# An attention and expert layer on one core: the order of work in the front

## The chip, the cores and the metric

The kernel runs on one core of a Trainium2 chip. The metric is the device time of one execution in microseconds. The core has TensorE (PE in the profile; its weight loads are listed apart as PEld), VectorE (DVE), ScalarE (ACT), GpSimd (POOL) and SyncE (SP), which only issues transfers here. Each engine works through its own list of instructions in order and waits where data of another engine is missing. Transfers are issued from the queues of SP, ACT and POOL.

## What is computed

```python
xn = layernorm(x)                                   # x: 8 sequences x 1024 tokens x 256
# causal linear attention, 16 heads of 16
q = elu(xn @ Wq.T) + 1 ; k = elu(xn @ Wk.T) + 1 ; v = xn @ Wv.T
out = einsum(q, cumsum(k v)) / clip(einsum(q, cumsum(k)), 1e-6)
attn = out @ Wo.T
# 8 experts, the best 2 of each token
logits = xn @ Wr + br
weights, experts = top_k(logits, 2) ; weights = softmax(weights)
ffn = sum over the two of weight * (silu(xn @ W1[e]) * (xn @ W3[e])) @ W2[e]
result = x + attn + ffn
```

All is in float32. The experts run on gathered rows alone: a tile is 128 rows of one expert.

## The kernel before

**Blocks and tiles.** The 8192 tokens are 16 blocks of 512 (four chunks of 128). Attention goes block by block. The experts go tile by tile: the first 4 blocks (FB) make a first list of 25 full tiles (N1), so that expert work can start before all tokens are routed; the other tiles come from a second list.

**The front** is everything up to the first expert tile. It is written in one `manual_schedule` section (L1084 to L1169), in which VectorE, ScalarE, TensorE and GpSimd keep the order in which the program names their instructions. The work comes from generators: each `next(...)` issues the instructions up to the next `yield`. After the section the framework's planner chooses the order; `in_order` pins single instructions to the program's order.

**What the front does.** WARMING (L104) matmuls without use run first on TensorE (L1087). `first_moments(t)` (L284) makes the statistics of block t on VectorE (bn_stats L290, bn_aggr L292, variance plus epsilon L296), raises them to the power -0.5 on GpSimd (L297) and makes the negative mean times that (the column "less", L299). `normalise(t)` (L333) applies it, chunks 0 and 2 on VectorE and 1 and 3 on ScalarE, all four of block 3 on VectorE, all of later blocks on ScalarE. `turn(t)` (L349) transposes the block on TensorE (L358) and copies it out on ScalarE (L363). `logits(t)` (L372) multiplies by the router's weights. The logits of four blocks are copied, turned (L1113 to L1119) and added up in `add_logits` (lg_all, L389).

`route(0, FB)` (L412) finds the two best experts of each token on VectorE, counts on TensorE how many rows of an expert stand before each token (`cnt_ps`, L465), and from that gives every row its place in the lists (`slot`, L486). Then come the softmax weights (L490 to L494), which go into the table `tab`; the table is written to DRAM by a transfer on SP (L1192).

`first_batch()` (L634) turns places into lists. For each of 32 columns (16 chunks, first and second expert) a 128 x 128 mask is made that has a one, or the token's number, where a row's place is. The masks of the first experts are made on VectorE in groups of four (`at_places`, L593), those of the second on ScalarE (two passes each, L672 and L676) for columns 0 to 7 and on GpSimd (L652) for 8 to 15. TensorE sums them (`sum_ps`, L706); ScalarE copies the sums (`sums4`, L713), a small matmul folds them (L715), and `tokens` (L616) makes the row numbers on VectorE. GpSimd then gathers rows and table entries of each tile (`ffn_load`, L1214).

**Block 0's attention** is partly in the front: `project_q`, `project_k`, `project_v` (L816 to L857), with `elu1` (two ScalarE passes for the exponential, one VectorE combine), and `mask_q` (L827), which masks q for pairs of heads on ScalarE. Their results stand in four PSUM buffers of the pool `ps_mm`.

**Queues.** SP takes, in program order: blocks 0 to 3, the small weights, blocks 4 and 5, w2, copies of the turned blocks, acc copies of x, the table, then tile 0's weights (`ffn_weights`, L1283, two transfers of 512 KB), more acc copies, tile 1's weights, the blocks 6 and 7, wo, the blocks 8 and 9, then tile 2's weights and so on. The weights have five buffers, so the second half of tile 2's waits until tile 0's first half was used. From tile 1 on, SP reads the expert's number from `te_late`, a copy that GpSimd makes behind tile 0's gather. Blocks 6 to 15 are normalised later, two at a time (`moments(t, 2)`, L302): VectorE reads both blocks, and block t's `normalise` needs the result.

**After the front**, a loop over tiles j (L1389) does one `ffn_step` and some attention steps. `ffn_turn(j)` turns a tile's gathered and normalised rows on TensorE, `ffn_hidden` makes the gate and up products (`gu_ps`, L1307) and their combination hT, `ffn_out` multiplies by w2 (`y_ps`, L1326).

Of the kernel before, what the change touches and what calls it, by code (L numbers as in the profile page):

```python
# [46 lines left out]
F32 = mybir.dt.float32  # L47
# [7 lines left out]
P = 128  # L55
# [9 lines left out]
def tile_attention_moe(  # L65
# [38 lines left out]
    WARMING = 14  # L104
# [155 lines left out]
    nc.gpsimd.memset(va, 0.0)  # L260
# [3 lines left out]
    nc.gpsimd.memset(own_of, 0.0)  # L264
# [3 lines left out]
    nc.gpsimd.tensor_scalar(upto_neg, before, -1.0, None, ALU.add)  # L268
    base_row = iota("base_row", E, ROWS, 0, 0)

    for o in range(KC):
        nc.gpsimd.tensor_copy(own_of[:, o, o * HALF : (o + 1) * HALF], own)
# [11 lines left out]
    def first_moments(t):  # L284
# [3 lines left out]
        for c in range(NCH + 1):  # L288
            if c < NCH:
                nc.vector.bn_stats(st[:, c, :], xbs[t][:, c, :])  # L290
            if c > 0:
                nc.vector.bn_aggr(mv[:, c - 1, :], st[:, c - 1, :])  # L292
            if t == FB and c == 1:
                yield
# [111 lines left out]
    nc.gpsimd.memset(new, 1.0)  # L406
    nc.gpsimd.memset(new[:, :, 0:1], 0.0)
# [4 lines left out]
    def route(a, b):  # L412
# [40 lines left out]

        reset = new[:, :, 0:n]
# [18 lines left out]
        )  # L473
        yield
# [14 lines left out]
        den2 = work("den2", n)  # L489
        nc.vector.tensor_scalar(den2, diff, 1.0, None, ALU.add)  # L490
        wt = tab[:, tiles, 0]
        nc.vector.reciprocal(wt, den2)
        second = slice(NT + a * NCH, NT + b * NCH)
        nc.vector.tensor_tensor(tab[:, second, 0], diff, wt, ALU.mult)  # L494
        if a > 0:
            nc.vector.tensor_copy(tab[:, second, 1:3], tab[:, tiles, 1:3])
        yield
# [136 lines left out]
    def first_batch():  # L634
# [7 lines left out]
        late = FT - 2 * PART  # L642
# [3 lines left out]
        less_place = f_one.tile([P, late], F32, name="less_place")  # L646
        nc.scalar.mul(less_place, place[:, 1, 0:late], -1.0)
        place_f = f_one.tile([P, 2 * PART], F32, name="place_f")
        nc.gpsimd.tensor_copy(place_f, place[:, 1, late:FT])
        late_at = [masked.tile([P, PART, P], F32, tag="s_sb", name="late_at") for _ in range(2)]  # L650
        for i in range(2 * PART):
            nc.gpsimd.tensor_scalar(  # L652
                late_at[i // PART][:, i % PART, :], cols, place_f[:, i : i + 1],
                number1[:, FT + late + i : FT + late + i + 1], ALU.is_equal, ALU.mult,
            )
        upto = add_up(sizes(False), "upto1")
# [13 lines left out]
        mid_at = [masked.tile([P, PART, P], F32, tag="s_sb", name="mid_at") for _ in range(2)]  # L670
        for i in range(late):
            nc.scalar.activation(  # L672
                mid_at[i // PART][:, i % PART, :], cols, AF.Square,
                bias=less_place[:, i : i + 1],
            )
            nc.scalar.activation(  # L676
                mid_at[i // PART][:, i % PART, :], mid_at[i // PART][:, i % PART, :], AF.Relu,
                bias=number1[:, FT + i : FT + i + 1], scale=from_last[:, i : i + 1],
            )

# [9 lines left out]
        yield  # L690
        sum_ps = ps_y.tile([P, P], F32, tag="y", name="sum_ps")
        groups = [(late_at, 2), (None, 0), (mid_at, 0), (mid_at, 1), (None, 1), (late_at, 3)]
        groups += [(None, 2), (None, 3)]
        for n, (made, g) in enumerate(groups):
            if made is None:
# [4 lines left out]
            else:  # L700
                at = made[g % 2]
            if n == 1:
                yield
            for i in range(PART):
                c = N1 * ((0 if made is None else FT) + g * PART + i)
# [78 lines left out]
    def elu1(dst, z):  # L784

        neg = two.tile([P, TB], F32, tag="neg", name="neg")
# [40 lines left out]
    def mask_q(t, o):  # L827
        qT, qm = blocks[t][0:2]
        for a in range(2):
            nc.scalar.mul(qm[:, o, a, :], qT[:, o, :], par[:, a : a + 1])  # L830

    def project_kv(t, c, a):
        z = ps_mm.tile([P, 2, H], F32, tag="mm", name="zkv"[:2] + "kv"[a])
# [8 lines left out]
    def project_k(t, c):  # L842
# [3 lines left out]
            kn[:, c : c + 2, :].rearrange("p c h -> p (c h)"), z.rearrange("p c h -> p (c h)")  # L846
# [237 lines left out]
    with tc.manual_schedule(engines={EN.DVE, EN.Activation, EN.PE, EN.Pool}):  # L1084
# [9 lines left out]
        next(parts[0])  # L1094
        for t in range(FB):
            next(parts[t + 1])
            next(parts[t])
            normalise(t)
            if t == 2:
                nc.scalar.copy(lgT4[:, 0, :], lg_ps.pop(0))  # L1100
            turn(t)
# [6 lines left out]
            else:  # L1108
                lg_ps[t - 1] = logits(t - 1)
        next(parts[FB])  # L1110
        lg4 = ps_t.tile([P, FB * P], F32, tag="t", name="lg4")
        for t in range(1, FB - 1):
            nc.vector.tensor_copy(lgT4[:, t, :], lg_ps.pop(t))  # L1113
        for t in range(FB - 1):
            nc.tensor.transpose(lg4[:, bass.ts(t, P)], lgT4[:, t, :], ident)
        next(constants)
        next(parts[FB])
        nc.scalar.copy(lgT4[:, FB - 1, :], logits(FB - 1))
        nc.tensor.transpose(lg4[:, bass.ts(FB - 1, P)], lgT4[:, FB - 1, :], ident)  # L1119
# [5 lines left out]
        turn(FB)  # L1125
        routing = route(0, FB)
# [3 lines left out]
        next(qs[0])  # L1130
        next(routing)
        listing = first_batch()
        next(listing)
        next(listing)
        lg_t = logits(FB)
        ks = [project_k(0, c) for c in range(0, NCH, 2)]
        for k in ks:
            next(k)
        lgT = f_two.tile([P, P], F32, tag="lgT", name="lgT")
        nc.scalar.copy(lgT, lg_t)  # L1140
# [3 lines left out]
        next(routing)  # L1144
        next(vs[0])
        mask_q(0, 0)
# [348 lines left out]
```

## Time and profile before

| | us |
|---|---|
| median of 3 runs | 1266.21 (1262.2 to 1268.4) |
| the profiled execution, its own time | 1262.54 |
| its span, first to last instruction | 1260.7 |
| block 0 normalised, start | 9.71 |
| logits of four blocks added (lg_all), start | 21.91 |
| sums of the first list copied, start | 41.53 |
| tile 0's rows gathered, issue | 44.33 |
| first expert matmul (gu_ps L1307), start | 49.99 |
| block 6's rows read by VectorE, start | 54.81 |
| TensorE busy, 0 to 50 / 50 to 140 | 36.22 / 85.90 |
| TensorE busy, 500 to 1100 | 600.00 |

The profile is one execution. Times of instructions count from the start of the span. A group's line gives the line in the code, the engine, what is written and what is read, how often, the busy time and the idle time ahead of it with the instruction that ended it. The chain of waits is followed back from the last instruction, so it names at each moment the work for which the end was waiting. In a table of stages, each row gives a stretch of time, its length, the busy time of PE, PEld, DVE, ACT and POOL in it, the clock that TensorE was granted (1.00 is full), the DMA engines' share, and GB/s. A busy PE is not a PE at full clock.

### The profile page before, as it was taken

The numbers are of one execution on the slowest core, as the hardware profiler recorded it, in microseconds if no ns is written. First come the engines' busy times: TensorE is split into PE (matmuls) and PEld (weight loads), VectorE is DVE, ScalarE is ACT, GpSimd is POOL, SyncE is SP. The second block draws the span as 40 slices with busy tenths as digits, with TensorE's granted clock in tenths as the row PEclk, the third lists the DMA queues.
The fourth block names the chain that finished last, engine by engine and source line by source line (L and its number), as shares of the span: only waits on it lengthen the run. The fifth ranks groups of instructions, "written<-read, shape, count | busy, mean of one in ns | idle before, by whom it ended". The sixth has DMA issues, their size and how long they took to land.

```text
span 1260.7 us, 29753 instructions
## 1 busy us (share of the span) xinstructions
PE 1217.8 (97%) x11460; PEld 1058.2 (84%) x11460; DVE 674.5 (54%) x1541; ACT 560.9 (44%) x1068; POOL 522.2 (41%) x460
## 2 busy tenths in 40 slices
PE   7799999999999999999999999999999999999994
PEld 5578887787898989988888989989888889899884
DVE  7677589864354554545453545545453545445451
ACT  5666475461534526262624426262626344252620
POOL 4734233233334544443535444444443444443422
PEclk9899999999999999999999999999999999999998
DMA  9798565557788796979799797879896877969782
GB/s 334 278 288 255 174 192 118 181 157 224 212 191 196 173 235 155 228 176 219 161 196 207 164 224 155 219 180 207 184 215 161 197 193 168 218 157 231 166 177 35
DMA packets 203934, 245.84 MB, mean 195 GB/s; under 512 B 72946, under 2 KB 127858, under 8 KB 203506
## 3 DMA queue, kind: packets, MB, share of 16 engines
q1 hardware_dynamic: 161010, 191.79, 52.5%
q0 software_dynamic: 38032, 43.22, 24.2%
q10 hardware_dynamic: 4752, 8.91, 2.1%
q8 instruction: 94, 1.54, 0.5%
q14 instruction: 46, 0.38, 0.1%
HBM read 187.91 MB, written 44.29 MB: 184 GB/s over the span
## 4 chain that ended last, share of the span: by engine, by line
PE 87%; DVE 5%; ACT 3%; DMA 3%; issue 1%; POOL 0%; SPq 0%; POOLq 0%; DVEq 0%; ACTq 0%
PE gu_ps L1307 37%; PE y_ps L1326 17%; PE s_ps L937 5%; PE o_ps L974 5%; PE a_ps L1016 5%; PE zq L820 4%; PE zkv L836 4%; PE zkk L836 4%; PE o_ps L956 2%; DMA xb<-in_x_dram 1%; PE tp L358 1%; DMA out_dram<-y,dst_i 1%; PE tp L883 1%; PE lg_ps L378 1%; DMA out_dram<-at 1%
## 5 line engine op out<-in xcount | busy, mean ns | idle before, releaser
L1307 PE MATMUL gu_ps<-xgT,w 128*128 128x128 f32 x4224 | 509.3, 277 | 0.5 <-ACT xgT L1270 0.5
L1307 PEld LDWEIGHTS gu_ps<-xgT,w 128*128 128x128 f32 x4224 | 489.1, 192 | 20.0 <-issue 14.4
L1337 POOL DMA_INDIRECT out_dram<-y,dst_i x107 | 175.2, 1638 | 328.3 <-DVE s_sb L944 103.3
L1326 PE MATMUL y_ps<-w_sb,hT 128*128 x1056 | 251.0, 380 | 1.8 <-DVE hT L1318 1.6
L1217 POOL DMA_INDIRECT xg<-in_x_dram,src_i x132 | 129.1, 978 | 240.1 <-DVE half L1240 109.9
L1326 PEld LDWEIGHTS y_ps<-w_sb,hT 128*128 128x128 f32 x1056 | 190.4, 191 | 23.6 <-DVE hT L1318 2.0
L944 DVE TENSOR_TENSOR s_sb<-s_ps,causal 128x512 f32<-128x512 f32 x256 | 159.8, 682 | 81.5 <-PE s_ps L937 75.2
L1315 ACT ACTIVATE hT<-gu_ps 128x512 f32<-128x512 f32 x132 | 78.8, 597 | 277.1 <-PE gu_ps L1307 207.5
L1222 POOL DMA_INDIRECT entry<-tab_d,of_i x107 | 106.4, 995 | 42.3 <-issue 31.4
L1318 DVE TENSOR_TENSOR hT<-gu_ps,hT 128x512 f32<-128x512 f32 x132 | 90.3, 684 | 61.9 <-PE gu_ps L1307 33.0
L1240 DVE COPY half<-xg 128x512 uint16<-128x512 uint16 x105 | 47.5, 453 | 134.9 <-ACT xg L1230 134.9
L1333 DVE TENSOR_SCALAR y<-y_ps,entry 128x256 f32<-128x256 f32 x132 | 63.6, 482 | 99.8 <-PE y_ps L1326 99.5
L1021 ACT COPY at<-a_ps 128x256 f32<-128x256 f32 x64 | 23.8, 372 | 172.1 <-PE a_ps L1016 123.7
L937 PE MATMUL s_ps<-qm,kT 32*128 32x256 f32 x1024 | 85.4, 404 | 0.5 <-DVE hT L1318 0.4
L1258 ACT COPY xgT<-halfT 128x512 uint16<-128x512 uint16 x105 | 79.7, 759 | 6.5 <-DMA halfT<-half 6.5
L1230 ACT ACTIVATE xg<-xg,entry 128x256 f32<-128x256 f32 x132 | 78.6, 596 | 4.1 <-DMA entry<-tab_d,num_i 3.4
L1016 PE MATMUL a_ps<-wo_sb,oT 128*128 128x256 f32 x256 | 68.2, 387 | 3.0 <-DVE oT L991 2.7
L974 PE MATMUL o_ps<-s_sb,va 128*32 128x128 f32 x2048 | 69.9, 276 | 0.0
L974 PEld LDWEIGHTS o_ps<-s_sb,va 128*32 128x32 f32 x2048 | 52.3, 109 | 17.9 <-issue 15.3
L937 PEld LDWEIGHTS s_ps<-qm,kT 32*128 32x128 f32 x1024 | 50.6, 184 | 18.6 <-issue 9.3
L1337 POOL DMA_INDIRECT acc_d<-y,src_i x25 | 40.9, 1637 | 53.0 <-DVE y L1333 15.1
L836 PE MATMUL zkv<-wkv_sb,xnT 128*128 128x256 f32 x256 | 59.6, 386 | 0.0
(228 smaller groups left out, 1353.9 us busy)
## 6 DMA issues: line engine op xcount, KB each, us to landing
w<-in_w_dram SPq DMA_DIRECT2D x264, 512.0 KB
rden<-over SPq DMA_DIRECT2D x128, 64.0 KB
xnT<-xnT_d SPq DMA_DIRECT2D x15, 512.0 KB
out_dram<-at POOLq DMA_DIRECT2D x13, 512.0 KB
out_dram<-in_x_dram SPq DMA_DIRECT2D x12, 512.0 KB
xnT_d<-xnT ACTq DMA_DIRECT2D x11, 512.0 KB
xb<-in_x_dram SPq DMA_DIRECT2D x9, 512.0 KB
w_sb<-in_w_dram SPq DMA_DIRECT2D x4, 1024.0 KB
```

The lines of the kernel that those rows point to most:

```text
L836: nc.tensor.matmul(z[:, i, :], lhsT=xnTs[t][:, k, bass.ts(c + i, P)], rhs=wkv_sb[:, k, a, :], start=(k == 0), stop=(k == KC - 1),)
L937: nc.tensor.matmul(s_ps[r][:, hh].rearrange("p a l -> p (a l)"), lhsT=kT[rows, hh, span], rhs=qm[rows, hh, :, span], start=True, stop=True,)
L944: last_masked[0] = nc.vector.tensor_tensor(sm, s_ps[r].rearrange("p k a l -> p (k a) l"), causal_b, ALU.mult)
L974: nc.tensor.matmul(o_ps[32 * r : 32 * r + 32, hh, :], lhsT=va[:, c, 4 * hh + r, a, :], rhs=s_sb[r][:, 2 * hh + a, :], start=(first and a = ...
L1016: nc.tensor.matmul(a_ps, lhsT=oT[:, hh, :], rhs=wo_sb[:, hh, :], start=(hh == 0), stop=(hh == 1),)
L1217: rows = nc.gpsimd.indirect_dma_start(out=xg[j], out_offset=None, in_=x_rows[:, :], in_offset=bass.IndirectOffsetOnAxis(ap=src_i[:, i : i ...
L1222: nc.gpsimd.indirect_dma_start(out=entry[j], out_offset=None, in_=table[:, :], in_offset=bass.IndirectOffsetOnAxis(ap=num_i[:, i : i + 1], ...
L1258: nc.scalar.copy(xgT[j].bitcast(U16).rearrange("p k (l b) -> p b k l", b=2), halves.pop(j).rearrange("p (b k) l -> p b k l", b=2),)
L1307: done = nc.tensor.matmul(ps[:, i, :], lhsT=w13[:, k, bass.ts(i, P)], rhs=xgT[j][:, k, :], start=(k == 0), stop=(k == KC - 1),)
L1318: nc.vector.tensor_tensor(hT, gu[1], hT, ALU.mult)
L1326: done = nc.tensor.matmul(y_ps, lhsT=hT[:, i, :], rhs=w2_sb[:, bass.ds(e * (IC * H) + i * H, H)], start=(i == 0), stop=(i == IC - 1),)
L1337: nc.gpsimd.indirect_dma_start(out=rows[:, :], out_offset=bass.IndirectOffsetOnAxis(ap=dst_i[:, i : i + 1], axis=0), in_=ys.pop(j), in_off ...
```

## The change

Nothing that is computed changes. It moves instructions of the front, and changes where some are made:

- WARMING is 18 instead of 14. Eight memsets, copies and conversions that GpSimd made early (va, own_of, upto_neg, new) go into `later_constants()`, called behind the last power.
- `first_moments` now pauses at chunk 2 of every block. Block 0's power is asked for at once and block 0 is normalised ahead of block 1's statistics; later blocks are normalised between the two parts of the next block's statistics. The copies of logits 1 and 2 stand in other places, and logits 3 come ahead of the turning of logits 2.
- The softmax weights are made while the counts run.
- Of the second experts' masks, GpSimd makes columns 8 to 14 and VectorE column 15.
- The exponentials of k follow ScalarE's masks, ahead of the sums; their scratch is the tile of kT. The sums are summed and copied in one piece, ahead of value copies, lgT's copy and the silu table load. q's combines follow the row numbers on VectorE. `mask_q` of block 0 follows the turning of tile 0.
- Four matmuls without use follow block 4's turn; 14 narrow ones (128 columns) replace the 3 wide ones (512) before the first tile.
- On SP, only block 6 is loaded behind tile 1's weights; blocks 7, 8 and 9 follow the weights of tiles 2, 3 and 4, and wo follows block 7.
- The transposes of tile 1's rows are pinned in order.

```diff
-    WARMING = 14
+    BY_ACT = 8
+    BY_POOL = 15
+    WARMING = 18
...
-            if t == FB and c == 1:
+            if c == NCH - 2:
                 yield
...
-    nc.gpsimd.memset(new, 1.0)
-    nc.gpsimd.memset(new[:, :, 0:1], 0.0)
+    def later_constants():
+        nc.gpsimd.memset(new, 1.0)
+        nc.gpsimd.memset(new[:, :, 0:1], 0.0)
+        nc.gpsimd.tensor_scalar(upto_neg, before, -1.0, None, ALU.add)
+        nc.gpsimd.memset(own_of, 0.0)
+        for o in range(KC):
+            nc.gpsimd.tensor_copy(own_of[:, o, o * HALF : (o + 1) * HALF], own)
+        nc.gpsimd.memset(va, 0.0)
...
+        if a == 0:
+            weights_of()
         yield
...
+        for i in range(BY_ACT, BY_POOL):
+            at_one(nc.gpsimd, made[i // PART][:, i % PART, :], FT + i, place_p[:, i : i + 1])
...
-        groups = [(late_at, 2), (None, 0), (mid_at, 0), (mid_at, 1), (None, 1), (late_at, 3)]
-        groups += [(None, 2), (None, 3)]
+        groups = [(1, 2), (1, 0), (0, 0), (0, 1), (1, 1), (0, 2), (0, 3), (1, 3)]
...
-        z = ps_mm.tile([P, 2, H], F32, tag="mm", name="zkv"[:2] + "kv"[a])
+        if t == 0 and a == 1:
+            z = ps_t.tile([P, 2, H], F32, tag="t", name="zv")
+        else:
+            z = ps_mm.tile([P, 2, H], F32, tag="mm", name="zkv"[:2] + "kv"[a])
...
         next(parts[0])
+        next(parts[0])
         for t in range(FB):
-            next(parts[t + 1])
+            if t > 0:
+                next(parts[t + 1])
             next(parts[t])
             normalise(t)
+            if t == 0:
+                next(parts[t + 1])
             if t == 2:
                 nc.scalar.copy(lgT4[:, 0, :], lg_ps.pop(0))
+            elif t == FB - 1:
+                nc.vector.tensor_copy(lgT4[:, 1, :], lg_ps.pop(1))
+            next(parts[t + 1])
             turn(t)
...
+        later_constants()
+        nc.vector.tensor_copy(lgT4[:, 2, :], lg_ps.pop(2))
+        next(constants)
         next(parts[FB])
         lg4 = ps_t.tile([P, FB * P], F32, tag="t", name="lg4")
-        for t in range(1, FB - 1):
-            nc.vector.tensor_copy(lgT4[:, t, :], lg_ps.pop(t))
-        for t in range(FB - 1):
+        for t in range(2):
             nc.tensor.transpose(lg4[:, bass.ts(t, P)], lgT4[:, t, :], ident)
...
+        def keep_busy(n, *cols_of):
+            for _ in range(n):
+                idle_ps = ps_mm.tile([P, TB], F32, tag="mm", name="idle_ps")
+                nc.tensor.matmul(idle_ps[:, 0:P], lhsT=ident, rhs=causal, start=True, stop=True)
+
+        keep_busy(4)
         routing = route(0, FB)
         next(routing)
         next(qs[1])
         next(routing)
-        next(qs[0])
         next(routing)
         listing = first_batch()
+        ks = [project_k(0, c) for c in range(0, NCH, 2)]
         next(listing)
         next(listing)
+        next(ks[0])
+        next(ks[1])
         lg_t = logits(FB)
-        ks = [project_k(0, c) for c in range(0, NCH, 2)]
-        for k in ks:
-            next(k)
-        lgT = f_two.tile([P, P], F32, tag="lgT", name="lgT")
-        nc.scalar.copy(lgT, lg_t)
         vs = [project_v(0, c) for c in range(0, NCH, 2)]
         next(vs[0])
         next(listing)
-        next(routing)
+        next(listing)
+        for q in qs:
+            next(q)
+        next(constants)
+        next(vs[1])
+        lgT = f_two.tile([P, P], F32, tag="lgT", name="lgT")
+        nc.scalar.copy(lgT, lg_t)
+        nc.scalar.activation(warm, ones[:, 0:1], AF.Silu)
+        for k in ks:
+            next(k)
         next(vs[0])
-        mask_q(0, 0)
-        next(listing)
-        next(qs[1])
-        next(constants)
-        next(listing)
-        nc.scalar.activation(warm, ones[:, 0:1], AF.Silu)
-        mask_q(0, 1)
         next(vs[1])
...
         attend_upto(3, False)
-
-        for _ in range(3):
-            idle_ps = ps_mm.tile([P, TB], F32, tag="mm", name="idle_ps")
-            nc.tensor.matmul(
-                idle_ps, lhsT=ident, rhs=blocks[0][0][:, 0, :], start=True, stop=True
-            )
+        keep_busy(14)
         next(routing)
...
+        if j < 3:
+            load_x(FB + 3 + j, nc.sync)
+        if j == 0:
+            in_order(nc.sync.dma_start(out=wo_sb, in_=woT.rearrange("(k p) o -> p k o", p=P)))
...
     ffn_turn(0)
+    for o in range(KC):
+        mask_q(0, o)
     ffn_weights(1)
-    for t in range(FB + 2, FB + 6):
-        load_x(t, nc.sync)
-        if t == FB + 3:
-            in_order(
-                nc.sync.dma_start(out=wo_sb, in_=woT.rearrange("(k p) o -> p k o", p=P))
-            )
+    load_x(FB + 2, nc.sync)
```

## The prediction

> **What bounds the kernel now.** I read the page's totals first, then the chain that ended last in its first 60 us, the engines' timelines of that stretch, and the table of stages for clock and busy time.
>
> ```profile
> span 1260.7 us, 29753 instructions
> PE 1217.8 (97%) x11460; PEld 1058.2 (84%) x11460; DVE 674.5 (54%) x1541; ACT 560.9 (44%) x1068; POOL 522.2 (41%) x460
> ```
>
> TensorE (PE) is busy 97% of the span. Between 60 and 1226 us it hardly waits, so what the front saves reaches the end one for one, and nothing else in this change can. The chain through the front (start, length, what):
>
> ```profile
> 1.83 5.79 DMA xb<-in_x_dram
> ...
> 9.71 0.42 DVE xb L338
> ...
> 10.17 0.65 PE tp L358 x3
> ...
> 21.91 0.30 DVE lg_all L389
> ...
> 39.08 0.63 ACT neg L788
> ...
> 40.41 1.23 ACT qm L830 x2
> 41.64 0.17 ACT sums L713
> ...
> 47.01 7.77 DMA xb<-in_x_dram
> 54.81 0.43 DVE st L312
> ```
>
> Three places matter. Block 0 is normalised at 9.71, after block 1's statistics (7.64 to 9.60), though its own variance was done at 5.69. The sums of the first list are complete at 39.32 and copied only at 41.53, because ScalarE first does a second exponential pair, a value copy and a masking of q. And VectorE stands from 51.3 to 54.81 for block 6's rows, with block 5's last step queued behind. What that does to PE (stage: length, busy time by engine, granted clock, DMA share, GB/s):
>
> ```profile
> 39.32:41.85 2.53, 0.00 (x1) 0.00 (x0) 0.00 (x0) 2.51 (x8) 0.00 (x0) 1.00 0.45 159
> 42.10:45.55 3.45, 3.45 (x11) 2.66 (x11) 1.84 (x6) 2.43 (x4) 2.42 (x3) 0.55 1.04 398
> 54.45:55.99 1.54, 0.00 (x2) 0.00 (x1) 1.18 (x3) 0.65 (x2) 1.24 (x2) 1.00 1.08 391
> 55.99:59.11 3.12, 2.54 (x8) 1.58 (x9) 3.12 (x11) 3.12 (x7) 2.81 (x2) 0.51 1.08 379
> 59.11:65.43 6.32, 6.32 (x50) 5.10 (x50) 5.88 (x29) 1.46 (x4) 2.60 (x3) 0.70 1.06 402
> ```
>
> PE idles, and right after each idle stretch the granted clock falls to about half.
>
> **Part 1, statistics and constants.** Block 0's power now follows its variance: ready at 5.69, POOL is free because the 3.1 us of constants (va 1.79, upto_neg 0.55, and smaller ones) go behind the powers. Power 1.01 to 1.05, less 0.16: normalising starts at about 7.1 instead of 9.71. The warm-up grows by 4 matmuls of two passes; warm passes take 0.11, cold ones 0.23, so it ends at 7.5 to 8.0 and no longer leaves the 3.5 us gap, after which the clock was 0.50 (12 to 14 us). But VectorE sets the pace afterwards: it starts on block 1 at 7.8, each block costs 2.7 (statistics and variance 1.94, less and normalising 0.76) as before, and three rather than two chunks of block 4 now come ahead of block 3's normalising. That starts at 16.4 to 17.0, against 16.68: nothing won by then. What is won is on PE behind it: block 3's turn, the logits and the turned logits are no longer queued behind late work. I get lg_all at 20.8 instead of 21.91: **-1.1**, bounds -0.5 and -1.6. Added wait: normalising block t waits for a power that has only half a block of statistics (1.25) as cover against 1.09; if the cover fails, three blocks pay some 0.1 each, inside the bounds. The constants then run from 20 to 23 on POOL, and upto_neg is wanted by the counts at 25.
>
> **Part 2, routing.** The three weight instructions (0.16, 0.26, 0.19) move into the wait for the counts, where q's combine (0.67) stood: 0. Without that cover they cost 0.6. The table's DMA no longer waits until 35.81, and SP is freed. The 4 busy matmuls (0.9) fall into PE's gap from 24.46 to 26.31: 0; at half clock (1.8) they fill it just.
>
> **Part 3, the first list.** Everything shifts by -1.1. VectorE gains one conversion (0.17) and one mask (0.3); its four row masks end at about 36.3, the new one at 36.6. ScalarE's eight pairs end at 35.25 (36.36 less 1.1). POOL makes seven masks instead of eight. These took 0.82 each until VectorE's 800-element comparison began at 32.78, then 0.9 to 1.8; four or five fast and the rest slow give 36.5, all fast 34.4. The Trainium skill ("SBUF — State Buffer", section "SBUF: two separate sides") says that VectorE with two SBUF inputs and GpSimd lock each other out for a whole instruction, and so speaks against giving the two more work side by side. The trace agrees for POOL (1.80 at most), not for VectorE (the 512-element masks took 0.68 to 0.70 each); by the rule and by the fast rows the sum below is the same.
>
> The sums are complete at 37.1. Their copy is not quite "at once": both k pairs (1.24 each) precede it on ScalarE, 35.25 + 2.48 = 37.7 instead of 41.53. That is **-3.8** in all, of which -2.7 here; bounds -3.0 and -4.4 (PE's end at 37.1 is the floor). Gathers, te_late and the later weight loads follow the copy by the same steps (0.76 to the numbers, 0.49 to POOL): the first rows land at 44.2 instead of 48.0. The first weights are issued when the early buffers are free, at 37.1 instead of 39.35. The q masks (2.7 on ScalarE) move behind tile 0's turned rows and run while PE computes tile 0 for 3.8; without that cover they would delay tile 1's rows by up to 2.7.
>
> **Part 4, bridging.** The q, k combines and kn's turn end on PE at about 42.7. 14 narrow matmuls follow, in front of tile 0's turn: 28 x 0.11 = 3.1, to 45.8; tile 0's rows are ready at 44.8. So the first gu_ps starts at 46.6 against 49.99, **-3.4**; without them -4.1, and at 0.23 a pass (6.4) only -0.1.
>
> **Part 5, block 6's rows.** Only this load now stands between tile 1's weights and tile 2's; x7, wo, x8 and x9 go behind later weights. SP issues tile 1's weights at about 42.2 (46.02 less 3.8). From that to landing took 8.8 before; with fewer transfers at once I take 7, bounds 5.5 and 8.8: 49.2, where VectorE arrives at 47.4. From there its work to block 6's turn took 67.59 - 54.81 = 12.8 and goes on in order, giving 62.0 to 62.3, **-5.3**; bounds -3.8 (landing 51) and -7.4 (VectorE never waits, 60.2). PE itself could be there at 59.6. x7, issued when tile 0's gate half is done (48.6), has until 55; at 8.8 it lands at 57.4 and costs 2.4. x9 goes out at about 66 and is read at 72: 0 to 3. I count both 0, as most transfers here landed faster than x6 did.
>
> **Sum.** 1262.54 for the profiled execution (span 1260.7 and 1.8 around it) less 5.3 is 1257.2. Three runs had the median 1266.21, 3.7 above the profiled one, so the median after is **1261**. Its own range is 1258 to 1263. Less than 0.5% (6.3 us) can't be told from no change here: the runs before span 6.2.
>
> **Rivals.** *All of the second wait goes (1257.5).* If x6 lands by 47.4, VectorE gives -7.4, and the half clock from 56 to 62.7 is gone; PE's own account (59.6 for 67.59) gives -8.0, to which tighter stages at 80 to 90 us (1.1 idle) can add: -7.4 to -9.5. For it: only 1.57 MB (tile 1's weights and x6) must land in 5 us, at the 390 GB/s shown. Against it: the gathers share the engines.
>
> *Bridging costs what it saves (1264).* If the idle second at 37 drops the clock, the 14 matmuls take 6.4 and gu_ps starts at 49.9; the earlier x6 keeps -1 to -3. Against: from 33.92 to 39.32, PE was busy 3.16 of 5.40 and kept clock 1.00. The Trainium skill ("TensorE: Matmul & The Clock Gate", section "What's actually happening") puts the drop after an idle window of about 3.4 us; the trace differs, since 1.54 us without a matmul was enough at 54.45. By the page this rival would be gone.
>
> *Slower (1272).* x7, x8 and x9 now queue on SP behind weights that wait for a buffer, and VectorE reads them in order, ahead of the hT products that PE needs. x6's lateness cost about 5.3: 2.0 of idle PE and half of the 6.7 us at half clock. If all three are that late, 16 less 5.3 makes +10, so some 1272 to 1276. It decides from a landing 12 us or more after the issue. Against: 8.8 was the worst.
>
> **Chances.** Forecast 0.40 (0.14 of it beyond 0.5%), all of the wait gone 0.32, bridging 0.12, slower 0.16 (0.02 of it within 0.5%). So faster 0.14 + 0.32 = 0.46; same 0.26 + 0.12 + 0.02 = 0.40; slower 0.14. The range 1254 to 1268 holds the first three with the runs' spread and the edge of the last.
>
> **What would show it.** Block 0 normalised at 7.1; lg_all at 20.8; the sums copied at 37.7; first gu_ps at 46.6; VectorE's wait for x6 under 2 us; block 6 turned at 62; full clock from 42 to 46 and from 52 on. The forecast is wrong if gu_ps starts after 49, if VectorE stands for x7 or x9, or if PE waits more than before between 300 and 1226 us (2.3 from 300 to 500).

## The result, and the profile after

The changed kernel took 1270.85 us (median of 19 runs, 1264.8 to 1277.23), the kernel before 1264.95 (19 runs, 1261.54 to 1274.27). The ratio is 1.0043, 95% interval [1.0029, 1.0057]: slower by about 5.5 us, which is little, but clear of the interval and in the other direction than the forecast of 1261. Here and below, the ratios come from executions in the chip's faster state alone and are not the quotients of the medians beside them, from which they differ by up to 0.15%. The profiled execution took 1269.36 (its span 1267.4) against 1262.54.

From the page of the changed kernel, its totals:

```profile
span 1267.4 us, 29840 instructions
PE 1222.1 (96%) x11498; PEld 1061.9 (84%) x11498; DVE 676.0 (53%) x1543; ACT 560.1 (44%) x1068; POOL 522.1 (41%) x459
```

TensorE has 38 more passes and 4.3 us more busy time, and idles 2.4 more than before (45.3 against 42.9, the span less the busy time). The chain of waits through its front (start, length, what):

```profile
3.43 8.13 DMA wr_sb<-in_wr_dram
11.69 0.65 PE lg_ps L374 x16
...
21.63 0.30 DVE lg_all L385
...
39.09 0.20 DVE num_i L628
...
41.13 5.01 DMA xg<-in_x_dram,src_i
46.23 0.61 ACT xg L1258
...
47.78 2.07 PE gu_ps L1337 x16
```

The front did get shorter: the first gu_ps starts at 47.78 instead of 49.99. What follows is not the work of the front. VectorE's timeline, with the idle time ahead in brackets:

```profile
7.08 0.74 DVE L334 TENSOR_SCALAR xb<-xb,tab 128x256 f32<-128x256 f32 x2
...
52.24 0.43 DVE L308 BATCH_NORM_STATS2 st<-xb 128x6 f32<-128x256 f32 x1 [1.17 <-DMA xb<-in_x_dram]
...
57.28 0.75 DVE L308 BATCH_NORM_STATS2 st<-xb 128x6 f32<-128x256 f32 x2 [1.70 <-DMA xb<-in_x_dram]
...
79.66 0.43 DVE L308 BATCH_NORM_STATS2 st<-xb 128x6 f32<-128x256 f32 x1 [6.06 <-DMA xb<-in_x_dram]
```

Before, there was one such wait for blocks 6 to 9, of 3.52 for block 6:

```profile
54.81 0.43 DVE L312 BATCH_NORM_STATS2 st<-xb 128x6 f32<-128x256 f32 x1 [3.52 <-DMA xb<-in_x_dram]
```

Now there are three: for block 6, for block 7 and, by far the longest, for block 9. The blocks are handled in pairs (`moments(t, 2)`), so block 6 can't be normalised before block 7 is read, nor block 8 before block 9. What it does to TensorE (same columns; first block 8's transposes in the kernel before, then the changed kernel):

```profile
86.08 0.93 PE L358 MATMUL tp<-ident,xb 128*128 128x128 f32 x4 [0.76 <-ACT xb L343]
```

```profile
63.60 0.44 PE L354 MATMUL tp<-ident,xb 128*128 128x128 f32 x2 [1.85 <-ACT xb L339]
...
78.85 1.99 PE L1356 MATMUL y_ps<-w_sb,hT 128*128 x8
80.77 0.70 PE L960 MATMUL s_ps<-qm,kT 32*128 32x256 f32 x4
86.60 0.69 PE L354 MATMUL tp<-ident,xb 128*128 128x128 f32 x2 [5.13 <-ACT xb L339]
87.22 1.22 PE L960 MATMUL s_ps<-qm,kT 32*128 32x256 f32 x2
```

TensorE idles 5.13 us ahead of block 8's transposes instead of 0.76, and what follows takes twice as long: two transposes 0.69 instead of 0.38, two passes of s_ps 1.22 instead of 0.69. The tables of stages say the same, first of the kernel before and then of the changed one (stretch, length, busy time of PE, PEld, DVE, ACT and POOL, granted clock, DMA share, GB/s):

```profile
80.00:90.00 10.00, 8.86 (x64) 6.67 (x62) 9.02 (x38) 6.19 (x13) 3.79 (x4) 1.00 0.88 250
90.00:100.00 10.00, 10.00 (x96) 8.29 (x95) 9.39 (x48) 7.46 (x15) 2.57 (x2) 1.00 0.89 311
```

```profile
80.00:90.00 10.00, 4.87 (x16) 2.25 (x15) 8.67 (x43) 3.57 (x6) 3.29 (x3) 0.82 0.83 248
90.00:100.00 10.00, 10.00 (x81) 8.28 (x81) 7.40 (x30) 6.06 (x11) 0.96 (x1) 0.84 0.61 203
```

Why block 9 is late stands in the timeline of SP's queue after the change (start, length, x how many):

```profile
43.81 0.46 SPq L154 DMA_DIRECT2D xb<-in_x_dram  x1
44.77 5.47 SPq L1318 DMA_DIRECT2D w<-in_w_dram  x2
50.29 0.46 SPq L154 DMA_DIRECT2D xb<-in_x_dram  x1
...
57.92 0.51 SPq L154 DMA_DIRECT2D xb<-in_x_dram  x1
59.27 10.06 SPq L1318 DMA_DIRECT2D w<-in_w_dram  x3
69.43 0.74 SPq L154 DMA_DIRECT2D xb<-in_x_dram  x1
```

SP stands in its weight transfers until an expert tile has freed a buffer (L1318, 10.06 us for three issues). Block 9 is queued behind them, goes out at 69.43 and lands at 79.64; before, all four blocks had been issued by 52.

How far the changed kernel leads (minus) or trails the one before, read off the starts of y_ps (L1356; L1326 before) of the same tile, in us:

| tile | 0 | 1 | 2 | 3 | 4 | 5 | 27 | 35 | 119 |
|---|---|---|---|---|---|---|---|---|---|
| before, start | 65.75 | 74.41 | 82.27 | 93.91 | 103.06 | 112.58 | 352.7 | 422.6 | 1144.7 |
| changed | -6.3 | -4.2 | -3.4 | +3.4 | +3.7 | +4.9 | +4.9 | +6.7 | +7.7 |

The lead of 3.4 turns into 3.4 behind at one tile, the one with the 5.13.

### The profile page after: what moved, and what is told of

The parts are those of the page before. It is cut to its first block, busy times and chain, and to the rows that moved or that the text cites. A ratio compares the mean times of both kernels' runs of the same rounds, so it can differ in the third digit from the quotient of the medians.

```text
span 1267.4 us, 29840 instructions
## 1 busy us (share of the span) xinstructions
PE 1222.1 (96%) x11498; PEld 1061.9 (84%) x11498; DVE 676.0 (53%) x1543; ACT 560.1 (44%) x1068; POOL 522.1 (41%) x459
## 3 DMA queue, kind: packets, MB, share of 16 engines
q8 instruction: 95, 1.56, 0.5%
## 4 chain that ended last, share of the span: by engine, by line
PE 82%; DVE 6%; DMA 6%; ACT 3%; issue 2%; SPq 1%; POOL 0%; POOLq 0%; DVEq 0%; ACTq 0%
PE gu_ps L1337 35%; PE y_ps L1356 15%; PE s_ps L960 5%; PE o_ps L997 5%; PE a_ps L1039 4%; PE zq L837 4%; PE zkv L858 4%; PE zkk L858 4%; PE o_ps L979 2%; DMA halfT<-half 2%; DMA xb<-in_x_dram 1%; PE tp L354 1%; PE tp L906 1%; DVE held L615 1%; DMA out_dram<-at 1%
## 5 line engine op out<-in xcount | busy, mean ns | idle before, releaser
L1356 PE MATMUL y_ps<-w_sb,hT 128*128 x1056 | 251.0, 380 | 2.1 <-DVE hT L1348 1.6
L1356 PEld LDWEIGHTS y_ps<-w_sb,hT 128*128 128x128 f32 x1056 | 190.4, 191 | 24.0 <-DVE hT L1348 2.0
L960 PE MATMUL s_ps<-qm,kT 32*128 32x256 f32 x1024 | 89.5, 408 | 2.8 <-DVE hT L1348 2.7
L858 PE MATMUL zkk<-wkv_sb,xnT 128*128 128x256 f32 x256 | 58.7, 380 | 0.0
```

What stands on the lines that cost most here:

```text
L858: nc.tensor.matmul(z[:, i, :], lhsT=xnTs[t][:, k, bass.ts(c + i, P)], rhs=wkv_sb[:, k, a, :], start=(k == 0), stop=(k == KC - 1),)
L960: nc.tensor.matmul(s_ps[r][:, hh].rearrange("p a l -> p (a l)"), lhsT=kT[rows, hh, span], rhs=qm[rows, hh, :, span], start=True, stop=True,)
L1356: done = nc.tensor.matmul(y_ps, lhsT=hT[:, i, :], rhs=w2_sb[:, bass.ds(e * (IC * H) + i * H, H)], start=(i == 0), stop=(i == IC - 1),)
```

## The experiments

The eighteen runs were made on five chips. Every ratio is against the kernel before on the same chip at the same time; on two chips (A and C) every kernel took longer.

| chip | kernel | us | ratio [95%] |
|---|---|---|---|
| A | before | 1287.08 | |
| A | loads_back | 1286.86 | 0.9990 [0.9957, 1.0024] |
| A | loads_back_wr | 1290.26 | 1.0017 [0.9987, 1.0048] |
| A | loads_late_alone | 1291.97 | 1.0034 [1.0003, 1.0065] |
| A | x_ahead | 1305.68 | 1.0156 [1.0118, 1.0195] |
| B | before | 1264.35 | |
| B | change_again | 1270.52 | 1.0042 [1.0021, 1.0064] |
| B | x7_late | 1269.77 | 1.0033 [1.0014, 1.0051] |
| B | x9_late | 1265.46 | 0.9994 [0.9974, 1.0015] |
| B | loads_back_no14 | 1266.55 | 1.0015 [0.9988, 1.0041] |
| C | before | 1284.68 | |
| C | before_pinned | 1288.69 | 1.0036 [1.0008, 1.0064] |
| C | loads_back_pinned | 1288.93 | 1.0025 [0.9992, 1.0058] |
| C | change_pinned | 1297.09 | 1.0104 [1.0066, 1.0141] |
| C | loads_back_again | 1287.35 | 1.0018 [0.9983, 1.0053] |
| D | before | 1264.78 | |
| D | groups_back | 1262.93 | 0.9984 [0.9965, 1.0003] |
| D | groups_no14 | 1260.67 | 0.9973 [0.9949, 0.9996] |
| D | groups_before | 1271.91 | 1.0061 [1.0038, 1.0084] |
| D | loads_back_no14_again | 1264.59 | 0.9996 [0.9972, 1.0021] |
| E | before | 1265.06 | |
| E | groups_no14_again | 1260.67 | 0.9967 [0.9949, 0.9985] |
| E | groups_no14_late | 1269.36 | 1.0029 [1.0012, 1.0046] |

### Are the loads the cause? (chip A)

`loads_back` is the change with the loads of blocks 6 to 9 and wo where the kernel before has them; `loads_late_alone` is the kernel before with the opposite edit and nothing else of the change.

```diff
-        if j < 3:
-            load_x(FB + 3 + j, nc.sync)
-        if j == 0:
-            in_order(nc.sync.dma_start(out=wo_sb, ...))
...
-    load_x(FB + 2, nc.sync)
+    for t in range(FB + 2, FB + 6):
+        load_x(t, nc.sync)
+        if t == FB + 3:
+            in_order(nc.sync.dma_start(out=wo_sb, ...))
```

> The changed kernel with one part undone: blocks 6 to 9 and wo are loaded in one go behind tile 1's weights again. Theory L (blocks 7 and 9 are late on SP's queue, VectorE waits for them in order, PE goes idle and its clock halves): VectorE no longer waits at 57 and 79 us, PE is busy over 8.5 of 10 us from 80 to 90, and the time falls below the kernel before, to 1258 to 1262 (the front's 2.2 us at the first gu_ps and the full clock from 56 to 63 remain). Rival P (the planner's other order behind the front, or the later q masks and pinned transposes, make the loss): still 1268 to 1272.

> The kernel before with that part alone: block 6 behind tile 1's weights; blocks 7, 8, 9 and wo behind the weights of tiles 2, 3 and 4. Theory L: the late blocks cost here what they cost in the changed kernel, some 8 to 10 us, less up to 3 because block 6 lands earlier: 1270 to 1276, with VectorE waiting for blocks 7 and 9. Rival P: within 2 us of before, 1263 to 1267.

The loads moved alone cost the kernel before 0.34%, about as much as the whole change costs (0.43%), though its interval goes down to 0.03%; VectorE waits 3.00 for block 7 there. With the loads put back no loss is left, but the gain that theory L expected does not show either. On this chip a second thing can hide it: TensorE's timeline of loads_back has the 14 bridging matmuls pulled apart, with "remote" as what ended the idle time.

```profile
42.81 2.15 PE L1160 MATMUL idle_ps<-causal,ident 128*128 128x128 f32 x16
...
49.53 0.49 PE L1160 MATMUL idle_ps<-causal,ident 128*128 128x128 f32 x2 [0.93 <-PE idle_ps L1160]
52.40 0.80 PE L1160 MATMUL idle_ps<-causal,ident 128*128 128x128 f32 x2 [2.37 <-remote]
```

They take from 42.81 to 54.45 where they took 3.3 us in the changed kernel's profile, and tile 0 starts at 57.2 instead of 47.8.

`x_ahead` is the change with the lines `load_x` and wo ahead of the step's weights.

> The changed kernel with blocks 7, 8, 9 each one step further ahead on SP: the load stands before the weights of the tile of that step, not behind them. Theory L: block 7 lands with block 6, block 9 some 7 to 10 us earlier than at 79.6, so most of both waits goes: 1259 to 1264. Rival P: 1268 to 1272.

It did the opposite of what it was meant to. The planner put block 9 behind eight `rden` transfers on SP: issued at 88.42, landed at 94.30, and TensorE idle for 8.17 ahead of 97.19. The profile names no releaser for this wait ("issue"). VectorE waits 5.21 for block 9 there, and behind it makes the s_sb copy (96.42 to 97.10) for which the same matmuls wait in loads_back, so the late block is the likely cause, but that is argued. The loss is the largest of all (1.56%); how much of it is the starved bridging was not tested.

`loads_back_wr` is loads_back with the router's weights loaded ahead of block 1.

> loads_back, and the router's weights are loaded ahead of block 1. Their landing at 11.56 held the first logits, and with them all of PE behind, for 1.83 us. If that is what took the front's gain up to lg_all, lg_all starts at 20.8 to 21.2 instead of 21.63 and the time is 0.4 to 0.8 us below loads_back; if VectorE sets the pace there, lg_all stays at 21.5 to 21.7. If the 256 short pieces of that load delay block 1, block 1's statistics start after 8.23 and lg_all comes later.

lg_all moved from 21.31 to 21.01 and the numbers of the first list (num_i) from 38.81 to 38.51. Behind that the bridging matmuls were starved again (until 51.9, and the first gu_ps only at 56.8), so the 0.3 us could not show in the time.

### Which load? (chip B)

`x7_late` and `x9_late` put all loads back except block 7's or block 9's, which stays behind the weights of its step. `loads_back_no14` is loads_back without `keep_busy(14)`; `change_again` is the change itself.

> The changed kernel itself, beside the next three on one chip. Theory L: 1.003 to 1.006 of before.

> The changed kernel with block 7 alone late: 6, 8, 9 and wo go behind tile 1's weights, block 7 stays behind tile 2's. Theory L with block 9 as the dear one: no wait at 81 to 86, a wait for block 7 of up to 3 us that costs at most 2: 0.998 to 1.001 of before. If any late load costs the whole: 1.003 or more.

> The changed kernel with block 9 alone late: blocks 6, 7, 8 and wo go behind tile 1's weights, block 9 stays behind tile 4's weights. Theory L, with block 9 as the dear one (5.1 us of idle PE at 81 to 86.6, then half clock): VectorE waits for block 9 as in the changed kernel, the wait for block 7 is gone, and the time is 0.3 to 0.5% above the kernel with all loads put back (0.999 of before), so 1.002 to 1.004 of before. If block 7 is the dear one: within 0.2% of 0.999.

> All loads put back and the 14 bridging matmuls left out. In the profile of the loads_back kernel these took from 42.8 to 54.7 us, in the changed kernel 43.1 to 46.4. Theory B (they delay tile 0 where TensorE's instructions come slowly): the first gu_ps starts at 47 to 48 and the time falls to 0.993 to 0.997 of before. Theory N (whatever stands there is slow in that stretch): the first gu_ps stays as late and the time is 0.998 to 1.001. Theory C (the clock needs them): gu_ps at half clock for 3 us, +1 to 2 us against loads_back.

The change repeated (1.0042). The expectation of the two single loads was the wrong way round: with block 7 alone late the kernel is 0.33% above the kernel before, with block 9 alone late level with it. (What each costs beside the kernel with all loads back and the 14 matmuls in is open, as that one did not run on this chip.) VectorE and then TensorE in x7_late, and VectorE in x9_late:

```profile
63.02 0.75 DVE L308 BATCH_NORM_STATS2 st<-xb 128x6 f32<-128x256 f32 x2 [8.62 <-DMA xb<-in_x_dram]
69.78 2.38 PE L354 MATMUL tp<-ident,xb 128*128 128x128 f32 x8 [5.12 <-ACT xb L339]
```

```profile
73.41 0.43 DVE L308 BATCH_NORM_STATS2 st<-xb 128x6 f32<-128x256 f32 x1 [2.74 <-DMA xb<-in_x_dram]
```

Which block is dear depends on the others. In x7_late block 7 goes out at 49.59, no later than in the change (50.29), but with blocks 8 and 9 and the weights in flight beside it, it lands 13.4 after its issue instead of 7.0; VectorE waits 8.62 instead of 1.70, and TensorE idles 5.12, as long as for block 9 in the change. In x9_late block 9 goes out at 64.98 instead of 69.43, and the 2.74 on VectorE leave TensorE no gap over 0.8. So it is not one transfer that is dear, but whichever lands too late for the pair that TensorE turns next, be it by its queue or by its flight.

loads_back_no14 was expected at 0.993 to 0.997 if the 14 matmuls were what hid the gain, and came to 1.0015. In its trace, TensorE is ahead of the kernel before until tile 4 (99.97 against 103.06) and behind it at tile 5 (113.53 against 112.58). There its order has the score matmuls one at a time between the transposes:

```profile
102.23 0.69 PE L960 MATMUL s_ps<-qm,kT 32*128 32x256 f32 x2
102.86 0.44 PE L354 MATMUL tp<-ident,xb 128*128 128x128 f32 x2
103.22 0.69 PE L960 MATMUL s_ps<-qm,kT 32*128 32x256 f32 x2
...
106.42 1.22 PE L960 MATMUL s_ps<-qm,kT 32*128 32x256 f32 x4
107.57 1.90 PE L997 MATMUL o_ps<-s_sb,va 128*32 128x128 f32 x32
```

The kernel before has eight passes together, in the time of two:

```profile
106.80 0.71 PE L937 MATMUL s_ps<-qm,kT 32*128 32x256 f32 x8
107.44 1.08 PE L974 MATMUL o_ps<-s_sb,va 128*32 128x128 f32 x32
```

One of these 32-row matmuls (two passes) holds TensorE for 0.62, and so do four (eight passes, 0.64). The Trainium skill ("TensorE: Matmul & The Clock Gate", section "Part 3: Packing small matmuls — row/col tiling") says that matmuls in different groups of rows run at the same time; the 0.64 for four agree, and a transpose between them takes that away.

### Is it the order on TensorE? (chips C and D)

First all transposes, logits and scores of block 0 were pinned in program order, in three kernels alike.

```diff
-                if t == FB + 1:
+                if t > FB:
                     in_order(done)
...
-                nc.tensor.matmul(
+                made = nc.tensor.matmul(
                     s_ps[r][:, hh].rearrange("p a l -> p (a l)"), lhsT=kT[rows, hh, span],
...
+                if t == 0:
+                    in_order(made)
...
-                nc.tensor.matmul(
+                done = nc.tensor.matmul(
                     lg_ps[32 * c : 32 * c + 32, :], lhsT=wr_sb[:, k, :],
...
+                if t > FB:
+                    in_order(done)
```

> The change with the loads of blocks 6 to 9 put back together, and with the transposes of x, the logits' matmuls and the scores' matmuls of block 0 held in program order on TensorE, so that the sixteen s_ps matmuls of a chunk stand together. Theory A (half of the loss is the order behind the front: lone s_ps matmuls take 0.62 us where four together take as long): sixteen s_ps take about 2.1 us instead of 4.3, the granted clock stays over 0.9 in 100 to 115, y to y between 100 and 113 takes about 10 us instead of 13.6, and the front's 2 to 3 us arrive at the end: 0.997 of before, some 1261. Rival B (whatever the front gains is given back later, because something else sets the end): the order looks as wanted, and the time is 1.000 or more. Rival C (eight transposes in one go make VectorE and ScalarE wait): a new idle stretch of 1 us or more behind the transposes, 1.002.

> The change as it is, its loads one per step behind the weights, with the same program order on TensorE as loads_back_pinned. Theory A with the loads' lateness as a cause of its own: block 7 lands about 57 and block 9 near 80 as in the change, TensorE idles 1.5 to 5 us in front of their transposes, and the time is 3 to 5 us above loads_back_pinned: about 1.0005 of before. Rival D (the loads only hurt because the planner's order follows them): within 1 us of loads_back_pinned. Rival E (the order has no part in it): 1.004, as the change.

> The kernel before with the same program order on TensorE: a control. Its scores already stand four and eight together, so Theory A has it at 0.999 to 1.001. If the program order by itself is worth something, it is below 0.998, and what loads_back_pinned gains is no gain of the front.

> The change with the loads of blocks 6 to 9 put back together, its only run so far having been on a slower chip (0.999 [0.9957, 1.0024] there, with the bridging matmuls starved). Theory A: the front reaches y of tile 2 some 3 us earlier than before, 2 to 4 us of it go where single s_ps matmuls stand between transposes, and the time is 0.9985 to 1.0005 of before. If the loads are the whole cause, it is 0.997 like loads_back_pinned.

The pinning was no clean test of the order: it cost the kernel before 0.36%, where none was expected, and loads_back_pinned, expected at 0.997, came to 1.0025. A likely reason is that transposes in one go wait for ScalarE (TensorE idles 1.24 us for its copies ahead of the logits in loads_back_pinned). The 14 matmuls were starved on this chip too, and loads_back_again (1.0018 [0.9983, 1.0053]) shows no gain. Of the loads the pinning says much, since the two kernels have nearly the same order on TensorE behind the front (of the first 1500 matmuls from the first gu_ps on, 12 stand elsewhere): late loads against loads put back are 1297.09 against 1288.93, 8.2 us, with intervals that do not touch (their traced executions are 3.2 apart). So rival D falls: the loads hurt by themselves, not through the order.

The second try only asks that the score matmuls of block 0 be issued behind the transposes of that step; all else is left to the planner.

```diff
                     in_order(done)
+                last_turned[0] = done
...
+                behind_turn = t == 0 and 4 * hh + r >= 0
+                with tc.issue_after(last_turned[0].ins) if behind_turn else ExitStack():
+                    nc.tensor.matmul(
                         s_ps[r][:, hh].rearrange("p a l -> p (a l)"), lhsT=kT[rows, hh, span],
```

> The change with its loads put back together, and with the scores' matmuls of block 0 issued behind the transposes of the block that is turned in that step, so that eight of them stand in two groups (6 and 2) instead of six. Theory A (the scattered score matmuls take back the front's gain): y to y behind 100 us is 10 to 11 us instead of 13.6, the clock stays at 1.00 there, and the time is 2 to 4 us under loads_back_no14_again on a chip that feeds the bridging matmuls, level with it on one that starves them. Rival B (something behind the front sets the end and takes any gain): the groups come together and the time does not move.

> As groups_back, and without the fourteen bridging matmuls, which a slow chip starves; the score matmuls stand in three groups. Theory A: 2 to 4 us under loads_back_no14_again, 0.997 to 0.999 of before. Rival B: level with loads_back_no14_again. Rival F (transposes in one go of eight wait for ScalarE's normalising, piece by piece): 0.2 us between them, 1 us or more in front of the logits, and half of the gain is gone again.

> The kernel before with the same constraint: a control. Its score matmuls stand in three groups as they did (2, 1 and 5), so theory A has 0.999 to 1.001; what it gains or loses is the price of the transposes in one go.

> The change with the loads put back and without the fourteen bridging matmuls, again, as the partner of groups_no14 on the same chip: 1.0015 on the chip of its first run, with 13.6 us between the y_ps of tiles 5 and 6. It is expected at 1.000 to 1.003 again, whatever the theory.

groups_no14 is 3.9 us under loads_back_no14_again, as theory A has it, but the two intervals overlap, so the worth of the grouping is not settled. groups_back, with the fourteen matmuls in, is 1.7 under it, and its interval takes in no change (0.9984 [0.9965, 1.0003]). groups_before was expected at no change and lost 0.61%: in the kernel before, the scores had covered a wait for block 8's normalising, and without them TensorE idled 1.82 and 1.12 between those transposes and ran the scores behind them at half clock. So the constraint by itself is no gain: it costs a front that is not ahead.

loads_back_no14_again showed something else. It is the same program as loads_back_no14, with the same order of all its matmuls from the first gu_ps on; here are the same instructions of its execution:

```profile
103.68 0.43 PE L374 MATMUL lg_ps<-xnT,wr_sb 128*32 128x128 f32 x8
104.03 0.70 PE L960 MATMUL s_ps<-qm,kT 32*128 32x256 f32 x4
104.66 1.08 PE L997 MATMUL o_ps<-s_sb,va 128*32 128x128 f32 x32
```

The clock stayed up here (o_ps 1.08) and fell there (1.90). From tile 4 to tile 5 it was 11.98 us here, 13.56 there and 9.52 before: some 2.5 of the loss go with the scattered scores (1.9 of them are three more groups of 0.62), and 1.6 are the clock, which fell in the one execution (chip B) and not in the other (chip D). It is not all that the clock did: between 60 and 1240 us the execution on chip B had the clock at half in five stretches of 3.4 or 6.8 us (from 82, 106, 232, 307 and 457), the one on chip D in none. They are 20 us together, by an estimate from that 10 us lost, and the two executions took 1272.55 and 1260.49, while the medians are 1266.55 and 1264.59. So the trace of one execution can't decide a question of 4 us in this kernel.

### The loads once more, on the best version (chip E)

groups_no14_late is groups_no14 with the loads as the change has them.

> The best version again: the change with its loads put back together, without the fourteen bridging matmuls, and with the scores' matmuls of block 0 behind the transposes. Expected 0.996 to 0.999 of before, if its first run was no accident; 1.000 or more if it was.

> As groups_no14_again, with the loads of blocks 7 to 9 and the weights wo left where the change puts them, one step's worth behind each step's weights. Theory A (the late loads are the larger half of the change's loss whatever the order): TensorE idles 1.5 us or more in front of block 7's transposes and 4 us or more in front of block 9's, the clock falls to a half behind the second, and the time is 4 to 10 us above groups_no14_again. Rival D (the loads hurt only through the order): within 2 us of it.

The best version held: 1260.67 again, 0.9967 [0.9949, 0.9985], which beats both kernels. With late loads it takes 1269.36, 8.7 us more, and its interval [1.0012, 1.0046] lies clear of the other. The order on TensorE is nearly the same (66 of the first 1500 matmuls stand elsewhere). TensorE's timeline of groups_no14_late, and then its stage from 80 to 90:

```profile
63.97 0.44 PE L356 MATMUL tp<-ident,xb 128*128 128x128 f32 x2 [0.87 <-ACT xb L339]
...
85.76 2.16 PE L356 MATMUL tp<-ident,xb 128*128 128x128 f32 x8 [4.00 <-ACT xb L339]
```

```profile
80.00:90.00 10.00, 5.85 (x34) 3.32 (x33) 8.47 (x41) 5.26 (x10) 3.69 (x3) 0.83 0.83 251
```

In groups_no14_again the same stage has 8.90 busy at clock 1.00. Block 9's part is as expected (4.00 of idle time, then half clock), block 7's smaller (0.87, where 1.5 was expected). The lead over the kernel before at the y_ps of tiles 0 to 5 and 119:

| tile | 0 | 1 | 2 | 3 | 4 | 5 | 119 |
|---|---|---|---|---|---|---|---|
| groups_no14_again | -4.9 | -4.1 | -4.9 | -4.8 | -5.6 | -3.5 | -2.3 |
| groups_no14_late | -5.4 | -3.9 | -2.5 | +1.3 | +0.5 | +2.6 | +2.1 |

The tile at which the lead is lost is the changed kernel's. These two executions are 4.5 us apart (1260.36 and 1264.83); the rest of the 8.7 between the medians lies in executions of which no trace was taken.

## Why the prediction was wrong, point by point

**Part 1 (lg_all at 20.8, -1.1): the mechanism right, the size off.** Block 0 was normalised at 7.08 (7.1 forecast) and the clock was 1.00 from 11 to 15 us. But lg_all came at 21.63, -0.3. The step left out the router's weights: an 8 KB transfer issued at 3.43 lands 8.13 later, and the earlier logits now wait 1.83 for it. That is part of the missing 0.8: loading them first moved lg_all by 0.3 (loads_back_wr). The other 0.5 was not tested.

**Part 2 (0): right.** No wait behind the weights shows in the chain.

**Part 3 (sums copied at 37.7, -3.8): right but for Part 1's error.** 38.35, -3.2. The masks on POOL took 8.09 for seven, a mixture of short and long ones (0.79 to 1.82) as forecast. The first rows landed at 46.18 instead of 44.2: of the 2.0, 0.65 is the sums', the rest the flight of the rows, 5.01 instead of 3.7; from the sums to the gather's issue it was 2.8 in both kernels.

**Part 4 (first gu_ps at 46.6, -3.4): half right.** 47.78, -2.2. The bridging took 3.3 (3.1 forecast) at full clock. That it can be starved, as on chips A and C, was in no bound.

**Part 5 is the step that failed.** Block 6 landed at 52.2, not 49.2 (9.4 after tile 1's weights went out, over my bound of 8.8). Its turn at 63.60, -4.0, stayed inside the bounds of -3.8 and -7.4, and is set by block 7, which landed at 57.28: the "at 8.8 it lands at 57.4" of the prediction, and its cost on TensorE was 1.85 (2.4 there). Then "x9 ... 0 to 3. I count both 0, as most transfers here landed faster than x6 did". Block 9 went out at 69.43 instead of 66, because SP stands in front of weights that wait for a buffer, took 10.2 to land, and cost 5.13 of idle TensorE and the half clock behind it: 6.9 us from tile 2 to tile 3. In the two pairs with nearly the same order late loads cost 8.2 and 8.7 in all. Counting a worst case at nothing because other transfers had been quicker was the mistake: these two were late at the issue already (50.29 for 48.6, and 69.43), and then flew for 7.0 and 10.2 behind weights that had just gone out.

**The sum.** A lead of 4.0 at block 6's turn instead of 5.3, 3.4 of it left at tile 2, then +6.9 from tile 2 to tile 3, and in smaller pieces +0.3, +1.2, +1.8 and +1.3 (tiles 4, 5, 31 and 112, with -0.3 in between), whose causes were not tested: 7.7 behind at the last tiles, 6.8 in the profiled executions' times and 5.9 in the medians. The premise that a gain in the front reaches the end one for one was too strong as well: in groups_no14_again 5.6 ahead at tile 4 are 2.3 at the last tiles.

**The rivals.** "Slower (1272)" named the mechanism, the place and very nearly the time (1270.85). I gave it 0.16, since "it decides from a landing 12 us or more after the issue". That threshold was wrong: 7.0 for block 7 and 10.2 for block 9 were enough, since the issue itself was late (x7_late, with 13.4 for block 7, is the case that the rival had described). "All of the wait goes" fell with block 6, which landed at 52.2 and not by 47.4. "Bridging costs what it saves" fell in the changed kernel's execution (3.3 at full clock); in loads_back on chip A the bridging took more than it could save, but first by standing idle, which this rival had not named.

**What was right after all.** With the loads put back, the scores behind the transposes and the fourteen matmuls left out, a gain arrives: 1260.67, -4.1 on chip D and -4.4 on chip E. The loss of the change is that of its moved loads, as the two pairs show; in the planner's own order the change and loads_back never ran on one chip. The rest of the change is worth some 4 us with the scores grouped and without the fourteen matmuls, and in the planner's own order its four runs lie between a gain of 1 and a loss of 2 (0.9990 to 1.0018, the fourteen matmuls in or out), none of them clear of no change.

## What to carry to other kernels

A transfer's lateness is the wait of its queue plus its flight: before moving a load behind others on a queue, look at what those wait for, and compare issue plus the slowest flight with the moment of its first reader. A block that is read in a pair is due when its partner is due. And where a planner orders what follows, a change at the front is also a change of that order: compare kernels in which the order is held the same, with a control, before putting a difference down to the edit.

## What the runs showed of the hardware that was not expected

- The clock fell without a gap in TensorE's work: at 105.9 us in loads_back_no14, behind some 4 us of single 32-row matmuls between transposes, with TensorE busy 3.40 of the 3.40 us ahead, and in another execution of the same program, on another chip, not at all. The Trainium skill ("TensorE: Matmul & The Clock Gate", section "What's actually happening") tells of an idle window of about 3.4 us that runs freely, so that the moment shifts from run to run. The shift agrees; that a window must be idle does not, as TensorE's records leave no idle time there.
- A lone 32-row matmul held TensorE nearly as long as four (0.62 against 0.64).
- On the two slower chips, the 14 small matmuls were starved (11.6 us in loads_back, instead of 3.3 in the changed kernel's profile and in groups_back), with "remote" and "issue" as what ended the idle time; the kernel before took 1.6 to 1.8% longer there than on the other three. Whether the two have one cause was not tested.
- 8 KB landed 8.13 us after the issue, behind block loads of 512 KB.
